# A two-level fast-multiplication block on one core: restores on ScalarE, x in seven transfers, x for results later

## The chip, the core and the metric

The kernel runs on one core of a Trainium2 chip. The core has a matrix engine (PE, TensorE), a vector engine (DVE, VectorE), an activation engine (ACT, ScalarE), a general engine (POOL, GpSimd) and SP (SyncE), which here only issues transfers. Each engine runs its own queue of instructions in order; semaphores tie the queues together. Transfers are issued by SP, ACT or POOL and carried out by DMA queues. The metric is the time on the device in microseconds, the lower the better. Three runs of the kernel before gave 2135.2, 2135.29 and 2135.4.

## The reference

x has 8 sequences of 1024 rows of 512 numbers, all float32. Cut to what matters:

```python
xn = layernorm(x)
# s: a decayed, causal product of features, three decay rates mixed by a softmax gate
q, gate = xn @ Wq, softmax(xn @ Wg)
for i in range(3):
    scores = (q @ (xn @ Wk[i]).T) * decay[i] ** expn * causal
    blended += gate[i] * (scores @ (xn @ Wv[i]))
s = blended @ Wo * out_scale
# g: a gated feed-forward part; every weight is one of 16 numbers, picked by an index
h = silu(xn @ lut[gate_idx].T) * (xn @ lut[up_idx].T)     # 1376 wide
g = silu(h @ lut[down_idx].T)
return x + s * g
```

## The kernel before

**Phase 1** works through the sequences 0 to 7. It normalizes x, computes the gated product in 8 chunks a sequence (`project`, `chunks`), and beside it builds the feed-forward weights. Everything that phase 2 needs is written to DRAM: the transposed xn of each sequence with some sums of its blocks (`xs_d`), the blended features (`bl_d`), and the weights with their sums (`quad_d`, `wgu_d`, `wd_d`, `wdl_d`, `wdt_d`).

**Phase 2** does the three feed-forward products and the result, one sequence after the other. Its products use the Winograd form of fast multiplication (7 products of half size instead of 8) on two levels: an outer step k in 1 to 7, and inside it an inner step i in 1 to 7. For each outer step the core holds seven planes of x in the tile `xs` (128 partitions, 7 outer steps, 7 planes, 256 columns): the four blocks B11, B12, B21, B22, loaded from `xs_d`, and three sums. POOL makes the sums (`sums_of_x`, L696), and one of them, B22 - B12, overwrites B12 in plane 1.

- `single` (L703 the weights `wr`, L713 the matmuls `fs`, `fsE`) computes the last 96 of the 1376 columns with plain blocks, in seven products on the outer level. In sequence 0 it comes first; in the others between the gate-up part and the down part.
- `quads` is the gate-up part: two rounds of seven nodes and then three nodes that pair two outer steps, (1, 6), (5, 7) and (2, 3), with `Fourth` for outer step 4. A `Node` loads its weights `wq` (L754, L757) into a ring of three slots, multiplies (L763), and DVE and ACT empty the four PSUM banks. `Fourth` has its weights `w` (L799) and matmuls at L806. `Fourth` and `single` use plain B12, so `restore` (L832) fetches it back from `xs_d`, one outer step for each transfer, issued by POOL: step 4 after the second round, then 1 and 6, 5 and 7, 2 and 3 behind the three pair nodes. In `after_57` and `after_23` POOL also makes sums and the multiplications of gate and up (L919), for half 1 of the columns first, then half 0.
- `down` has seven `DownNode`s in the order 1, 5, 6, 2, 7, 4, 3, whose weights `wdd` (L1009) come into the same ring. The matmuls at L1018 are its two-level part; those at L1029 multiply the rows left over (`wdl`, L1246), which the multiplications at L919 write. DVE makes the operand sums `z`, `sx`, `sy` (L986).
- The result: `tail` (L1125) adds the last 96 columns, `result` multiplies the blended features `fbl` (L1226) by Wo (L1132), DVE scales (L1134), POOL adds x (L1136), and the rows go out (L1137, by SP in the last sequence, else by POOL). This x comes into the tiles `gx` by `load` (L1082), four transfers of 256 KB for each half of the rows; half 1 takes the room of the pair nodes' tile `u2`, half 0 that of `e5`. `load` is called at the down nodes 5 (half 1) and 2 (half 0).
- While `down` runs, `beside` loads the x of the next sequence (L686), one outer step behind each node. Only the x of sequence 0 is loaded at once, 3.5 MB in one transfer, at the start of phase 2.

**What sets the order.** A scheduler orders the instructions when the program is built. `keep_order` binds PE, DVE, ACT and POOL to the order in which the code was traced; SP is left to the scheduler apart from the very start. So SP's queue can hold a transfer ahead of others that were traced before it, and as SP issues in order, a transfer whose room is not yet free holds all that stand behind it. Hardware-issued transfers share eight semaphores in turn, so one also waits until the transfer eight places before it has landed.

At the end of phase 1 SP stores `wdl_d` (L305, behind POOL's last weight sum, L303), and ACT stores the last `bl` (L580).

Of the kernel before, what the change touches and what calls it, by code (L numbers as in the profile page):

```python
# [20 lines left out]


ENGINES = (mybir.EngineType.PE, mybir.EngineType.DVE, mybir.EngineType.Activation, mybir.EngineType.Pool)


def keep_order(tc, seen, engines=ENGINES):

    last = {}
    order = mybir.DependencyInfo(mybir.DependencyClass.NoSync, mybir.DependencyReason.DATA)
    for i in tc.nc.cur_bb.bb.instructions:  # L30
        if i.name not in seen and i.engine in engines:
            if i.engine in last:
                tc.add_manual_dep(i, last[i.engine], order, reason="traced in this order")
            last[i.engine] = i.name
# [3 lines left out]
def recurrent_block(ctx: ExitStack, tc, x, wq, wk, wv, wo, wg, decay_logits, out_scale, lut, gidx, uidx, didx, out):  # L38
# [19 lines left out]
    nc = tc.nc  # L58
    B, T, V = x.shape
# [5 lines left out]
    NC = T // P  # L65
# [22 lines left out]
    xs_d = [dram.tile([P, 14, U], F32, name=f"xsd{b}", tag=f"xsd{b}") for b in range(B)]  # L88
# [37 lines left out]
    seen = {i.name for i in nc.cur_bb.bb.instructions}  # L126
# [532 lines left out]
    X_OF = {1: 0, 2: 1, 3: 2, 5: 3, 6: 4, 7: 5, 4: 6}  # L659
    D_OF = {1: 0, 7: 1, 2: 2, 3: 3, 5: 4, 6: 5, 4: 6}  # L660
    H = U // 2
    ORDER = (1, 6, 5, 7, 2, 3, 4)

    def phase_2():
        with (
# [19 lines left out]
            def load_x(b, xs, first=0, end=7):  # L685
                nc.sync.dma_start(  # L686
                    out=xs[:, first:end, 0:4, :],
                    in_=xs_d[b][:, 2 * first : 2 * end].rearrange("p (k r) (s t) -> p k (r s) t", r=2, s=2),
                )
# [136 lines left out]
            def quads(b, xs, h, sums, at_last):  # L826


                def restore(*ks):

                    for k in ks:
                        nc.gpsimd.dma_start(out=xs[:, X_OF[k], 1, :], in_=xs_d[b][:, 2 * X_OF[k], H:])  # L832

                def two(ap):
                    return ap.rearrange("p (a t) -> p a t", a=2)
# [46 lines left out]
                def pair_steps():  # L882

                    (p1, u2), (e5, u3) = (
                        (t[:, :, :H], t[:, :, H:])
                        for t in (tmp.tile([P, 4, U], F32, name=f"{k}{b}_l", tag=k) for k in ("p1", "u2"))
                    )
                    room[0] = u3

                    def of_h(half, n):  # L890
                        r, c = divmod(n, 2)
                        t = half * U + c * H
                        return h[:, 4 * NQ + r, t : t + H]

                    def node_16(t, n):
                        nc.scalar.copy(p1[:, n], t[n][:, :H])
                        nc.vector.tensor_tensor(u2[:, n], t[n][:, H:], p1[:, n], ALU.add)

                    def node_57(t, n):
                        nc.scalar.copy(e5[:, n], t[n][:, :H])  # L900
                        nc.vector.tensor_tensor(u3[:, n], t[n][:, H:], u2[:, n], ALU.add)
                        nc.gpsimd.tensor_tensor(u2[:, n], u2[:, n], e5[:, n], ALU.add)

                    def node_23(t, n):
                        nc.vector.tensor_tensor(p1[:, n], t[n][:, :H], p1[:, n], ALU.add)
                        nc.scalar.activation(of_h(0, n), p1[:, n], AF.Silu)
                        nc.vector.tensor_tensor(of_h(1, n), t[n][:, H:], u2[:, n], ALU.add)
                        nc.scalar.activation(of_h(1, n), of_h(1, n), AF.Silu)

                    def after_57():  # L910
                        for n in (0, 3, 1, 2):
                            nc.gpsimd.tensor_tensor(e5[:, n], e5[:, n], u3[:, n], ALU.add)
                        restore(5, 7)

                    def after_23():
                        restore(2, 3)
                        for half, other in ((1, e5), (0, u3)):
                            for n in (0, 3, 1, 2):
                                nc.gpsimd.tensor_tensor(of_h(half, n), of_h(half, n), other[:, n], ALU.mult)  # L919

                    yield (1, 6), node_16, lambda: restore(1, 6)
                    yield (5, 7), node_57, after_57
                    yield (2, 3), node_23, after_23
# [144 lines left out]
            def down(b, h, h_tail, bl, ahead, beside):  # L1068
# [4 lines left out]
                order = (1, 5, 6, 2, 7, 4, 3)  # L1073
# [5 lines left out]
                def load(half, pool, tag):  # L1079
                    xr[half] = pool.tile([P, 4, V], F32, name=f"gx{b}_{half}", tag=tag)  # L1080
                    for n in range(4):
                        nc.sync.dma_start(out=xr[half][:, n], in_=x[b, ts(4 * half + n, P), :])  # L1082

                def at(c, n):
                    return c[:, n // 2, n % 2]
# [44 lines left out]
                def result(k):  # L1130
                    ps = next_bank(f"ps{b}_{k}")
                    nc.tensor.matmul(ps, lhsT=bl[:, ts(k, P)], rhs=wo_sb, start=True, stop=True)  # L1132
                    g, o = of_chunk(k)
                    nc.vector.scalar_tensor_tensor(g, wide(ps), osc, g, ALU.mult, ALU.mult)  # L1134
                    end = (b, k) == (B - 1, NC // 2 - 1)
                    (nc.vector if end else nc.gpsimd).tensor_tensor(wide(o), wide(o), g, ALU.add)  # L1136
                    (nc.sync if b == B - 1 else nc.gpsimd).dma_start(out=out[b, ts(k, P), :], in_=o)  # L1137

# [3 lines left out]
                node.fifth_copy()  # L1142
                for i, k in enumerate(order):
                    following, todo = None, []
                    if k == 5:
                        load(1, tmp, "u2")
                    if k == 2:
                        load(0, tmp2, "e5")
                    if k == 6:
                        of[7], parts = sum_of(f"sx{b}_7", "sx", a11, a21, ALU.subtract)  # L1150
                        later = [p + (ALU.subtract,) for p in parts]
                    if k == 2:
                        of[3] = s2
                        later += [
                            (o, x1, o, ALU.subtract)
                            for o, x1 in zip(
                                (s2[0][:, 0:2], s2[0][:, 2:4], s2[1]), (a12[0][:, 0:2], a12[0][:, 2:4], a12[1])
                            )
                        ]
                    if k != order[-1]:  # L1160
                        kk = order[i + 1]
                        z, todo = four_of(f"z{b}_{kk}", of[kk])
                        following = DownNode(b, kk, of[kk], z)
                    if k == 1:
                        todo += first_sums
                    if k == 6:
                        todo += later[:2]
                        later = later[2:]
                    elif k in (2, 7, 4):
                        n = 2 if k == 2 else 1  # L1170
                        todo = later[:n] + todo if k == 4 else todo + later[:n]
                        later = later[n:]

                    def some(n):
                        vector_sums(todo, n)

                    empty = empties[k]
                    node.sixth()
                    some(1)
                    node.product(0, 2)  # L1180
                    node.rest(0)
                    empty(node.t, 0)
                    some(1)
                    if following:
                        following.first()
                    else:
                        tail(4, bank("s11", f"pd{b}_4"))
                    node.seventh()
                    some(1)
                    node.product(1, 3)  # L1190
                    node.rest(1)
                    empty(node.t, 1)
                    some(1)
                    if following:
                        following.fifth()
                        following.fifth_copy()
                    else:
                        tail(5, bank("sE", f"pd{b}_5"))
                    node.rest(3)
                    empty(node.t, 3)  # L1200
                    some(1)
                    node.product(2, 4)
                    node.rest(2)
                    empty(node.t, 2)
                    some(3)
                    node = following
                    beside(k)
# [4 lines left out]
                behind = 1 if b == B - 1 else 3  # L1212
# [5 lines left out]

            more = iter(())
            xs = room_for_x(0)  # L1220
            load_x(0, xs)
            for b in range(B):
                h = hp.tile([P, 2 * NK, T], F32, name=f"h{b}", tag="h")
                h_tail = hp.tile([P, T], F32, name=f"ht{b}", tag="ht")
# [27 lines left out]
                def beside(k):  # L1252
# [9 lines left out]
                    if n > 4:  # L1262
                        some(more, 4)

                down(b, h, h_tail, bl, got, beside)

    phase_1()
    phase_2()
    keep_order(tc, seen)


# [39 lines left out]
```

## Time and profile before

| | |
|---|---|
| time, median of 3 runs | 2135.29 us (2135.2 to 2135.4) |
| time of the profiled execution | 2137.89 us |
| its span, first to last instruction | 2136.1 us |
| mean granted PE clock | 0.996 |
| PE busy | 2113.7 us, 99% |
| PE weight loads busy | 1680.5 us, 79% |
| DVE, ACT, POOL busy | 1409.4, 930.1, 1054.8 us |
| moved by DMA | 361.45 MB, mean 169 GB/s |
| chain that ended last | PE 97%, DMA 1% |

Phase 1 takes the first 603.7 us. Sequence 0's gate-up part begins at 622.5, sequence 1's at 806.7, and from there a sequence takes 188.3 us. The last matmul ends near 2124.8 and the last addition of x at 2126.65. Some groups that the change touches (columns: line, engine, operation, tiles, count, then busy us and mean ns, then idle before and who ended it):

```profile
L696 POOL TENSOR_TENSOR xs<-xs 128x256 f32<-128x256 f32 x224 | 171.2, 791 | 7.8 <-DMA bld<-bl 2.2
xs<-xsd SPq DMA_DIRECT2D x49, 512.0 KB, 7.2
gx<-in_x SPq DMA_DIRECT2D x64, 256.0 KB, 4.1
wq<-quadd SPq DMA_DIRECT2D x112, 896.0 KB, 4.5
wdd<-wdd SPq DMA_DIRECT2D x56, 896.0 KB, 4.7
```

The last four are from the page's list of transfers: tile, issuing queue, count, size of one, and the median time from issue to landing. "SPq" is SP's queue. A busy PE can hide a slow one: where PE has stood still, its clock is granted at half, which the stretches of the trace show as a lower granted clock.

### The profile page before, as it was taken

Reading aid. Unit: us, or ns where it says so; the run is one execution under the profiler, and the core shown is the slowest. Engines: PE = TensorE matmul, PEld = TensorE weight load, DVE = VectorE, ACT = ScalarE, POOL = GpSimd, SP = SyncE. Lnnn points to the kernel's source line nnn. Section 1 sums busy time; section 2 is a strip of 40 time slices with the busy share of each in tenths; the row PEclk is TensorE's granted clock in tenths of the full one; section 3 lists DMA queues with packets and bytes.
Section 4 is the critical chain, followed back from the end, with each engine's and each line's share of the span. In section 5 each row is a group of like instructions: output and inputs, shape, how many; then the busy total and the mean of one; then the engine's idle time right before and its main releaser. Section 6 shows DMA issues by size and latency. Waiting matters only on the chain.

```text
span 2136.1 us, 31153 instructions
## 1 busy us (share of the span) xinstructions
PE 2113.7 (99%) x11306; PEld 1680.5 (79%) x11306; DVE 1409.4 (66%) x2149; ACT 930.1 (44%) x2083; POOL 1054.8 (49%) x1103
## 2 busy tenths in 40 slices
PE   9999999999999999999999999999999999999997
PEld 5666666666668798888879888887978888797886
DVE  6889888669535675566567556655755665675566
ACT  3666666676434414423441442344144224414531
POOL 2654565353354627517552752655275265627532
PEclk9999999999999999999999999999999999999999
DMA  7555647574474544463454446445544644554451
GB/s 195 154 175 160 199 160 170 178 159 149 120 265 152 205 159 165 143 241 137 156 198 170 156 148 235 152 149 184 179 165 148 237 137 155 166 202 155 156 167 67
DMA packets 159183, 361.45 MB, mean 169 GB/s; under 512 B 52371, under 2 KB 83350, under 8 KB 158006
## 3 DMA queue, kind: packets, MB, share of 16 engines
q1 hardware_dynamic: 149606, 336.12, 48.6%
q0 software_dynamic: 7168, 22.03, 2.9%
q8 instruction: 90, 1.47, 0.3%
q10 hardware_dynamic: 2256, 1.32, 0.2%
q14 instruction: 63, 0.52, 0.1%
HBM read 282.87 MB, written 76.55 MB: 168 GB/s over the span
## 4 chain that ended last, share of the span: by engine, by line
PE 97%; DMA 1%; DVE 0%; POOL 0%; issue 0%; SPq 0%; ACTq 0%; ACT 0%; DVEq 0%; POOLq 0%
PE s L763 32%; PE pq L437 10%; PE pv L400 8%; PE sE L763 5%; PE s21d L1018 5%; PE s12d L1018 5%; PE s11d L1018 5%; PE po L565 4%; PE fs L713 3%; PE pd L1125 3%; PE ps L1132 3%; PE sEd L1018 2%; PE psc L543 2%; PE pu L551 2%; PE fsE L713 1%; PE pt L393 1%
## 5 line engine op out<-in xcount | busy, mean ns | idle before, releaser
L763 PE MATMUL s<-xs,wq 128*128 128x256 f32 x3264 | 731.4, 379 | 0.6 <-DMA wq<-quadd 0.6
L763 PEld LDWEIGHTS s<-xs,wq 128*128 128x128 f32 x3264 | 619.4, 190 | 96.9 <-issue 8.2
L437 PE MATMUL pq<-xnT,wqk_sb 128*128 128x512 f32 x512 | 230.3, 592 | 0.0
L786 DVE TENSOR_TENSOR s<-s,e 128x512 f32<-128x512 f32 x136 | 95.2, 700 | 204.0 <-ACT s L785 204.0
L1096 POOL TENSOR_TENSOR cu<-cu 128x256 f32<-128x256 f32 x32 | 35.1, 1098 | 312.3 <-DVE cl L1095 312.3
L400 PE MATMUL pv<-wvg_sb,xnT 128*128 128x387 f32 x512 | 177.6, 489 | 0.6 <-DMA wvg_sb<-in_wv 0.6
L696 POOL TENSOR_TENSOR xs<-xs 128x256 f32<-128x256 f32 x224 | 171.2, 791 | 7.8 <-DMA bld<-bl 2.2
L790 DVE TENSOR_TENSOR sE<-s,e 128x512 f32<-128x512 f32 x136 | 95.1, 699 | 105.9 <-PE s L763 105.9
L437 PEld LDWEIGHTS pq<-xnT,wqk_sb 128*128 128x128 f32 x512 | 92.4, 190 | 92.1 <-issue 91.8
L853 POOL TENSOR_TENSOR u<-u,e 128x512 f32<-128x512 f32 x64 | 80.0, 1271 | 149.2 <-DVE u L849 130.1
L379 POOL TENSOR_SCALAR rstd<-rstd 128x1 f32<-128x1 f32 x56 | 29.5, 526 | 228.6 <-ACT junk L378 227.8
L781 ACT COPY e<-sE 128x512 f32<-128x512 f32 x136 | 79.7, 586 | 138.5 <-PE sE L763 138.5
L763 PE MATMUL sE<-xs,wq 128*128 128x256 f32 x544 | 139.6, 379 | 0.0
L400 PEld LDWEIGHTS pv<-wvg_sb,xnT 128*128 128x128 f32 x512 | 92.7, 190 | 55.1 <-issue 2.7
L774 ACT COPY s<-s 128x512 f32<-128x512 f32 x136 | 77.5, 570 | 109.8 <-PE s L763 106.0
L785 ACT COPY s<-s 128x512 f32<-128x512 f32 x136 | 77.5, 570 | 97.8 <-PE s L763 97.8
L1018 PE MATMUL s12d<-wdd,z 128*128 128x128 f32 x896 | 118.6, 275 | 0.0
L763 PEld LDWEIGHTS sE<-xs,wq 128*128 128x128 f32 x544 | 103.4, 190 | 14.1
L1018 PEld LDWEIGHTS s12d<-wdd,z 128*128 128x128 f32 x896 | 109.3, 192 | 0.2 <-ACT s12d L1040 0.2
L857 POOL TENSOR_TENSOR h<-h,u 128x512 f32<-128x512 f32 x64 | 79.8, 1278 | 46.7 <-DVE u L864 46.5
L206 DVE TENSOR_SCALAR leaf<-idx,lut_x,lut_sb 128x1024 int32<-128x1024 int32 (+2 forms) x119 | 101.2, 876 | 0.0
L545 DVE TENSOR_TENSOR pr<-psc,w_tab 128x384 f32<-128x384 f32 x64 | 35.6, 556 | 92.3 <-PE psc L543 92.2
(237 smaller groups left out, 4292.1 us busy)
## 6 DMA issues: line engine op xcount, KB each, us to landing
wq<-quadd SPq DMA_DIRECT2D x112, 896.0 KB, 4.5
wdd<-wdd SPq DMA_DIRECT2D x56, 896.0 KB, 4.7
xs<-xsd SPq DMA_DIRECT2D x49, 512.0 KB, 7.2
wq<-quadd SPq DMA_DIRECT2D x48, 448.0 KB, 3.8
x<-in_x SPq DMA_DIRECT2D x64, 256.0 KB, 5.9
xsd<-ts SPq DMA_DIRECT2D x8, 2048.0 KB, 8.6
gx<-in_x SPq DMA_DIRECT2D x64, 256.0 KB, 4.1
out<-gx POOLq DMA_DIRECT2D x56, 256.0 KB, 2.3
```

Of the source, the lines that this page charges most:

```text
L206: nc.vector.tensor_scalar(o.bitcast(I32), iv, lut_x[:rows, k, :], lut_i[:rows, k, 0:1], ALU.bitwise_and, ALU.bitwise_xor,)
L400: nc.tensor.matmul(pv, lhsT=xnT[:, v, ts(c, P)], rhs=wvg_sb[:, v, :], start=(v == 0), stop=(v == NV - 1))
L437: nc.tensor.matmul(pq, lhsT=wqk_sb[:, v, ts(j, D)], rhs=xnT[:, v, ts(hf, U)], start=(v == 0), stop=(v == NV - 1))
L565: nc.tensor.matmul(po, lhsT=lh, rhs=rh, start=(n == 0), stop=(n == len(prods) - 1))
L696: nc.gpsimd.tensor_tensor(o, x1, x2, ALU.subtract)
L713: nc.tensor.matmul(ps, lhsT=w[:, 2 * W_OF[k] + n, :m], rhs=xs[:, X_OF[k], 2 * n : 2 * n + 2, :], start=start and n == 0, stop=stop and n == 1,
L763: nc.tensor.matmul(self.t[n][:, ts(a, H)], lhsT=self.w[:, a, (0, 1, 6, 2, 3, 4, 5)[i - 1], :], rhs=self.xs[:, X_OF[self.ks[a]], D_OF[i], : ...
L786: nc.vector.tensor_tensor(self.t[1], self.t[1], self.e, ALU.add)
L790: nc.vector.tensor_tensor(self.t[3], self.t[2], self.e, ALU.add)
L853: nc.gpsimd.tensor_tensor(o[:, n], o[:, n], other[:, n], ALU.add)
L857: nc.gpsimd.tensor_tensor(of_h(half, n), of_h(half, n), two(other[:, n]), ALU.mult)
L1018: nc.tensor.matmul(self.t[n][:, ts(a, P)], lhsT=self.lhs[i][:, e, ts(a, P)], rhs=self.w[:, e, D_OF[i], :], start=start and a == 0 and e == ...
```

## The change

It has five parts. `restore` issues from ACT's queue and fetches two outer steps in one transfer, by a slice with a step. In `after_23` half 0 is multiplied before half 1. The x of sequence 0 is loaded in seven transfers in the order in which `single` uses them. `load` is called at the down nodes 7 and 4 instead of 5 and 2, and a new function, `keep_behind`, binds these transfers behind what was traced before them on SP. In the last sequence the additions of x for results 2 and 3, not for 3 alone, are on DVE.

```diff
+def keep_behind(tc, seen, names):
+
+    last = None
+    order = mybir.DependencyInfo(mybir.DependencyClass.NoSync, mybir.DependencyReason.DATA)
+    for i in tc.nc.cur_bb.bb.instructions:
+        if i.name not in seen and i.engine == mybir.EngineType.SP:
+            if last and i.name in names:
+                tc.add_manual_dep(i, last, order, reason="behind what was traced before")
+            last = i.name
...
                 def restore(*ks):
 
-                    for k in ks:
-                        nc.gpsimd.dma_start(out=xs[:, X_OF[k], 1, :], in_=xs_d[b][:, 2 * X_OF[k], H:])
+                    some_of = slice(X_OF[ks[0]], X_OF[ks[-1]] + 1, max(X_OF[ks[-1]] - X_OF[ks[0]], 1))
+                    there = xs_d[b].rearrange("p (k r) t -> p k r t", r=2)
+                    nc.scalar.dma_start(out=xs[:, some_of, 1, :], in_=there[:, some_of, 0, H:])
...
                     def after_23():
                         restore(2, 3)
-                        for half, other in ((1, e5), (0, u3)):
+                        for half, other in ((0, u3), (1, e5)):
...
                     for n in range(4):
                         nc.sync.dma_start(out=xr[half][:, n], in_=x[b, ts(4 * half + n, P), :])
+                        held.add(nc.cur_bb.bb.instructions[-1].name)
...
-                    end = (b, k) == (B - 1, NC // 2 - 1)
+                    end = b == B - 1 and k in (2, 3)
                     (nc.vector if end else nc.gpsimd).tensor_tensor(wide(o), wide(o), g, ALU.add)
...
-                    if k == 5:
+                    if k == 7:
                         load(1, tmp, "u2")
-                    if k == 2:
+                    if k == 4:
                         load(0, tmp2, "e5")
...
             xs = room_for_x(0)
-            load_x(0, xs)
+            for k in (1, 6, 5, 2, 7, 3, 4):
+                load_x(0, xs, X_OF[k], X_OF[k] + 1)
...
+    held = set()
     phase_1()
     phase_2()
+    keep_behind(tc, seen, held)
     keep_order(tc, seen)
```

The sequences of instructions on PE, DVE, ACT and POOL are otherwise the same before and after; what changes beside these lines is SP's order, which the scheduler makes.

## The prediction

> **What bounds the kernel now.** I read the busy times first: PE is busy for 2113.7 of 2136.1 us, so what can be won is PE's 22.4 us of idleness and the time after each stall in which PE runs at half clock. Then the stretches say where these lie. Columns: stretch, its length, busy us of PE, PEld, DVE, ACT, POOL, granted clock, DMA share, GB/s.
>
> ```profile
> 603.70:622.30 18.60, 14.96 (x29) 5.55 (x30) 2.06 (x3) 4.51 (x7) 9.95 (x16) 0.82 0.78 300
> 719.90:752.20 32.30, 27.83 (x182) 24.41 (x181) 22.62 (x37) 9.30 (x25) 16.30 (x19) 0.95 0.77 281
> 1560.80:1749.10 188.30, 188.30 (x1049) 158.80 (x1049) 116.52 (x190) 71.08 (x141) 97.14 (x105) 1.00 0.51 172
> 1749.10:1938.20 189.10, 188.50 (x1049) 158.67 (x1049) 116.52 (x190) 71.07 (x141) 97.08 (x104) 1.00 0.50 172
> ```
>
> A middle sequence has no idle PE at all (third row). So only four places count: the step from phase 1 to phase 2 (first row), the end of sequence 0's gate-up part (second), a slip of 0.8 us in sequence 6 (fourth), and the tail behind the last matmul. The view of PE's waits names what ended each stall (total, times, longest):
>
> ```profile
> PE fs L713 <- DMA bld<-bl: 3.7, 1, 3.7
> PE s11d L1018 <- DMA wdd<-wdd: 2.9, 1, 2.9
> ...
> PE s L806 <- DMA w<-wgud: 0.9, 1, 0.9
> PE s11d L1029 <- POOL h L919: 0.6, 1, 0.6
> PE s L763 <- DMA wq<-quadd: 0.6, 1, 0.6
> ```
>
> The first name misleads: POOL's first sum of x starts at the same instant (607.33), so it is the landing of xs, 12.9 us after its issue. The chain of waits shows what a stall costs besides its idle time (start, length):
>
> ```profile
> 607.36 6.51 PE fs L713 x8
> 613.87 1.72 PE fsE L713 x4
> 615.59 3.43 PE fs L713 x8
> ```
>
> Eight matmuls took 6.51 us instead of 3.43: another 3.1 us. The other stall did the same (PE's timeline), where eight such matmuls elsewhere take 0.89:
>
> ```profile
> 746.05 1.84 PE L1018 MATMUL s11d<-wdd,sy 128*128 128x128 f32 x8 [2.94 <-DMA wdd<-wdd]
> 747.69 1.91 PE L1018 MATMUL s21d<-wdd,z 128*128 128x128 f32 x8
> ```
>
> **A. x of sequence 0 in seven transfers.** The edit is meant to take away 3.7 + 3.1 = 6.8 us. What decides is SP's queue, which issues in order:
>
> ```profile
> 594.06 0.56 SPq L686 DMA_DIRECT2D xs<-xsd  x1
> 605.19 0.33 SPq L305 DMA_DIRECT2D wdld<-wgu  x1
> 605.69 0.33 SPq L1245 DMA_DIRECT2D wdt<-wdtd  x1
> 606.07 1.32 SPq L754 DMA_DIRECT2D wq<-quadd  x1
> 610.45 0.32 SPq L1226 DMA_DIRECT2D fbl<-bld  x1
> 610.81 0.43 SPq L1246 DMA_DIRECT2D wdl<-wdld  x1
> 611.29 0.63 SPq L754 DMA_DIRECT2D wq<-quadd  x1
> ```
>
> In the changed program's SP order the seven transfers are not together. Four (k = 1, 6, 5, 2) stand where the one stood; then comes the store wdld, which waits for POOL's last weight sum (605.16); then k = 7, 3, 4; then fbl, whose room is free only when wdld has landed; then wdt, wdl, and only then the first gate-up weights wq, which stood ahead of fbl before. So 1.5 MB of x that crossed between 601 and 605 now crosses after 605, and the first wq is issued near 611 instead of 606.07.
>
> Working: the four transfers land by about 602.5 (2.1 MB behind the rest of wr, by the 0.30 to 0.41 MB per us of the DMA rows from 594 on). PE ends phase 1 at 603.67 and waits only for ACT's copy of bl (603.96), so it starts near 604.2 with no loss of clock. The seven products of single, 1.72 us each (row 613.87), are 12.0; the fifth needs x7. wdld moves from about 606.3 to 609.2 (0.92 MB at the 0.3 MB per us it had); the three x at 0.4 follow to 613.1, landing some 1.2 us behind their bytes: x7 at 611.6 against a need at 611.1. single ends near 616.8. Then fbl, wdt, wdl, wq are 2.56 MB at 0.39 MB per us (3.10 MB in 610 to 618): last byte 619.7. Transfers here landed 1.0 (xs) to 2.6 us (the first wq) behind their bytes by the same count; so wq lands at 620.7 to 622.3, I take 621.3. PE idles 4.5 us in front of its first gate-up matmul instead of 3.7 in front of single, and its clock drops again.
>
> Here a rule weighs in. The Trainium skill, "TensorE: Matmul & The Clock Gate" (What's actually happening), says the clock halves after an idle window of about 3.4 us and returns after about as long a busy one: a loss of 1.7 us. The rows say 3.1 after 3.69 us of idleness and 1.7 after only 2.94, below the rule's limit, so a shorter stall would not escape either. By the rule A ends at 621.3 + 1.7, by the first row at 621.3 + 3.1; before, the first gate-up matmul came at 622.46 at full clock. I take 2.4: A = **+1.2 us** (ends -0.8 and +2.9). The stall is moved, not removed.
>
> A second rule speaks against splitting: "DMA: Bandwidth & Descriptors" (Rules for kernel authors) asks for 1 MiB or more in a transfer, and its fit (Anatomy of one DMA) has 2.0 us fixed for each; in sequence, six more would cost 12 us. But from 745 to 750 this queue moved 414 GB/s out of transfers of 512 and 896 KB issued back to back, as much as out of the one large x (416 from 598 to 604), so I cost the split itself at nothing.
>
> **B. x for results later, multiplications of half 0 first, restores on ACT (sequence 0).** From 624.18 to 807.61 sequence 0 needs 183.43 us; a middle sequence without single is 188.29 - 12.04 = 176.25. So 7.2 us are lost. (1) w was issued at 719.16, behind four gx loads that waited for POOL's multiply until 717.24. It now stands before them and goes when its ring slot is free, near 715 as in sequence 1 (7.6 us ahead of use, 2.1 to land): -1.2. (2) L1029 waited for POOL's half 0: 0.6 idle. It goes, but restore (2, 3) now sits on ACT just before the copy L1040 that PE's third step needs, at 0.35 (ACT's issue of bld): -0.3. (3) The third wdd was issued at 739.08, behind gx loads waiting for POOL until 737.25. It now follows the second near 728.5, needed at 740.8, landing 4.7 to 6.8 after issue: -3.1 idle and -1.7 clock. Late next is the second wdd: its slot is w's, free near 727.7, landing 4.6 later at 732.3, needed at 732.6; it may cost up to 1. Sum: **-6.2** (ends -7.2 and -4.5).
>
> **C. The other seven sequences.** gx moves some 10 us later, past two wdd, and still lands over 20 us before its use; PE is full, so 0. POOL loses seven issues (0.74 + 1.13 + 2.19 us in sequence 0), for which nobody waits there. ACT gains four of 0.35 each; every wait they carry (weights in use, earlier restores, long-landed x) is already met, and the gap before the copy L785 behind them is 0.55 to 0.62: 0. Without that cover PE waits, as the third rival says. The slip in sequence 6 is one wq that took 8.2 us instead of 4.9 beside the same stores as before; I count half of its 0.8: **-0.4** (ends -0.8, +0.8).
>
> **D. Last sums on VectorE.** After the last matmul DVE ran L1134 for results 2 and 3 to 2125.62 and one add of 1.00 to 2126.65, beside POOL's add. Now 0.8, 0.69, 0.8, 0.69 from 2124.01, with POOL idle: 2127.0. The last add is 0.35 later, the store before it 0.6 earlier: **+0.2** (-0.1, +0.4).
>
> Sum: 1.2 - 6.2 - 0.4 + 0.2 = **-5.2 us**, made against the profiled execution (2137.89, span 2136.1), which lies 2.6 above the median of 2135.29. The same gain gives **2130.1 us**.
>
> **Rivals.**
> - *A wins as meant* (wq lands before single ends): -6 instead of +1.2, near 2122.9. For it: PE could start at 604.2. Against: SP's order and 2.56 MB in front of wq. 0.12.
> - *Half of B is lost again*, by the second wdd landing over a microsecond late behind restores and x of the next sequence, with a clock drop: -3 instead of -6.2, near 2133.3. 0.17.
> - *ACT is held by its restores.* An issue above the 0.55 us gap delays PE 32 times. At 1.0 us each, 0.45 x 32 = 14 us: 2144. It outweighs the gain from 0.72 us each, and reads as slower from 0.85. For it: POOL's issues took 0.56 to 0.74. Against: ACT's own row, 0.35. 0.08.
> - The forecast: 0.63, its own range 2127.3 to 2133.
>
> What this kernel's measurement can tell is about 0.2%, 4.3 us, so below 2131.0 is faster. Of the forecast's 0.63 some 0.46 lies there, with 0.12 of the first rival: 0.58. Slower: 0.08 and a little for the unforeseen, 0.09. The range 2125.5 to 2134 leaves out most of the first rival and the third.
>
> **What would show it.** A: fs starts near 604.2, and PE's waits name wq at the gate-up matmul (L774 of the changed file) with 4 to 5 us, with slow matmuls behind; were that wait absent, A is wrong. B: no wait on w, wdd or h in 715 to 750. C: middle sequences of 188.3; if longer, look at ACT. D: the last add ends 0.3 later.

## The result, and the profile after

The changed kernel took 2136.33 us (median of 14 runs, 2134.48 to 2139.82), the kernel before 2135.35 in the 14 runs beside it (2132.47 to 2138.97). The ratio is 1.0002, with a 95% interval of 0.9994 to 1.001: no difference that can be measured. The forecast was 2130.1. The profiled execution has a span of 2135.2 us (before 2136.1) and a mean clock of 0.999.

That nothing moved does not mean that nothing happened. PE's waits in the changed kernel (who waited for what at which line: us in total, times, longest; lines of the changed file, 11 and more above those of before):

```profile
PE fs L724 <- DMA xs<-xsd: 11.1, 8, 2.0
PE s L774 <- DMA wq<-quadd: 4.0, 1, 4.0
PE warm L352 <- POOL nhalf L141: 1.4, 1, 1.4
PE s12d L1030 <- ACT s12d L1052: 0.8, 1, 0.8
PE fs L724 <- ACT bl L577: 0.4, 1, 0.4
```

The waits for wdd, w and h in sequence 0 are gone, and so is the one in front of `single` of sequence 0. The 4.0 us for wq is the stall that the forecast saw move. The first line is new: `single` waits for its x, once in sequence 0 (0.15 us) and in each later sequence for a restore (10.9 us in all). The stretches show what that makes of a sequence (columns as in the prediction; the step to the gate-up part, sequence 0, sequence 1):

```profile
603.34:623.92 20.58, 16.10 (x38) 7.37 (x38) 2.75 (x4) 5.09 (x8) 17.38 (x26) 0.92 0.96 357
623.92:801.35 177.43, 176.59 (x1022) 154.29 (x1021) 115.85 (x186) 68.05 (x136) 81.27 (x76) 1.00 0.49 170
801.35:991.33 189.98, 188.50 (x1050) 158.71 (x1049) 116.52 (x190) 71.08 (x141) 93.19 (x98) 1.00 0.50 172
```

A middle sequence took 188.30 with PE never idle; now it takes 189.98, and PE is busy for 188.50 of it.

Set stage against stage, the two profiled executions give this. A stage ends where the row names it; "gate-up" is the first block of 20 matmuls of the gate-up part, which comes four matmuls of each kind into it.

| stage | before, us | after, us | difference | forecast |
|---|---|---|---|---|
| phase 1, to its last matmul's end | 603.66 | 603.35 | -0.3 | 0 |
| A: from there to gate-up of sequence 0 | 20.52 | 20.57 | +0.05 | +1.2 |
| B: sequence 0 | 183.43 | 177.43 | -6.0 | -6.2 |
| C: sequences 1 to 7, to the last matmul's end | 1317.15 | 1328.72 | **+11.6** | -0.4 |
| D: from there to the end of the last add | 1.89 | 2.11 | +0.2 | +0.2 |
| from there to the end of the span | 9.45 | 3.02 | **-6.4** | 0 |
| sum | 2136.1 | 2135.2 | -0.9 | -5.2 |

So there are two large terms that the forecast did not have, of opposite sign. One is in the seven later sequences, the other behind the last addition, where no engine computes any more.

**The first one, in sequence 1.** ACT's timeline of the changed kernel (start, length, instruction, idle time before it), where `single` begins at 905.71:

```profile
904.66 0.42 ACT L920 ACTIVATE h<-h 128x256 f32<-128x256 f32 x1
906.37 0.42 ACT L918 ACTIVATE h<-p_l 128x256 f32<-128x256 f32 x1 [1.30 <-DVE p_l L917]
906.70 0.42 ACT L920 ACTIVATE h<-h 128x256 f32<-128x256 f32 x1
906.79 0.37 ACTq L844 DMA_DIRECT2D xs<-xsd  x1
```

SP's timeline in the same stretch, and PE's (the products of `single`, two to a row of eight matmuls):

```profile
905.04 1.18 SPq L1021 DMA_DIRECT2D wdd<-wdd  x2
```

```profile
905.71 3.60 PE L724 MATMUL fs<-xs,wr 128*96 128x512 f32 x8
909.15 1.88 PE L724 MATMUL fsE<-xs,wr 128*96 128x512 f32 x4
912.50 3.64 PE L724 MATMUL fs<-xs,wr 128*96 128x512 f32 x8 [1.48 <-DMA xs<-xsd]
```

restore(2, 3) stands behind the last Silu in ACT's queue, and that Silu waits for DVE's `p_l`. So it goes out at 906.79, 1.1 us after `single` has begun, and it lands 5.6 us behind its issue (the view of tile `xs` in this stretch). Product 2 is the fourth of `single`, 12 matmuls in; PE is ready for it at 911.0 and gets it at 912.5. In the kernel before, POOL's timeline has the same transfers in good time:

```profile
906.01 2.79 POOL L912 TENSOR_TENSOR u_l<-u_l 128x256 f32<-128x256 f32 x4
908.73 2.19 POOL L832 DMA_DIRECT2D xs<-xsd  x4
910.93 1.42 POOL L919 TENSOR_TENSOR h<-h,u_l 128x256 f32<-128x256 f32 x2
```

There `single` began at 911.97, about 2 us after operand 2 had been issued, the restores landed in 2.3 to 2.5 us, and the two wdd went out behind them, at 911.30. In the changed kernel the two wdd are ahead, by 1.75 and 0.9 us. The experiments had to tell which part matters: the place in ACT's queue, the two wdd, or the two operands in one transfer.

### The profile page after: what moved, and what is told of

The parts are those of the page before. It is cut to its first block, busy times and chain, and to the rows that moved or that the text cites. A ratio compares the mean times of both kernels' runs of the same rounds, so it can differ in the third digit from the quotient of the medians.

```text
span 2135.2 us, 31120 instructions
## 1 busy us (share of the span) xinstructions
PE 2112.1 (99%) x11306; PEld 1678.7 (79%) x11306; DVE 1410.9 (66%) x2150; ACT 930.1 (44%) x2083; POOL 1021.3 (48%) x1046
## 3 DMA queue, kind: packets, MB, share of 16 engines
q10 hardware_dynamic: 9936, 8.66, 1.3%
## 4 chain that ended last, share of the span: by engine, by line
PE 97%; DMA 3%; DVE 0%; ACT 0%; issue 0%; SPq 0%; ACTq 0%; DVEq 0%
PE s L774 33%; PE pq L448 10%; PE pv L411 8%; PE sE L774 6%; PE s12d L1030 5%; PE s21d L1030 5%; PE s11d L1030 5%; PE po L576 4%; PE pd L1138 3%; PE ps L1145 3%; PE sEd L1030 2%; PE psc L554 2%; PE fs L724 2%; DMA xs<-xsd 2%; PE pu L562 2%; PE pt L404 1%
## 5 line engine op out<-in xcount | busy, mean ns | idle before, releaser
L785 ACT COPY s<-s 128x512 f32<-128x512 f32 x136 | 77.5, 570 | 114.3 <-PE s L774 110.9
L774 PEld LDWEIGHTS sE<-xs,wq 128*128 128x128 f32 x544 | 103.9, 191 | 14.3
```

Of the source, the lines that this page charges most:

```text
L774: nc.tensor.matmul(self.t[n][:, ts(a, H)], lhsT=self.w[:, a, (0, 1, 6, 2, 3, 4, 5)[i - 1], :], rhs=self.xs[:, X_OF[self.ks[a]], D_OF[i], : ...
```

## The experiments

Eleven kernels. A, B, C, D are the steps of the forecast. The kernel before ran beside them with medians of 2135.82, 2136.34 and 2135.83 us.

### 1. The restores back on POOL (e1_restore_pool)

```diff
-                    some_of = slice(X_OF[ks[0]], X_OF[ks[-1]] + 1, max(X_OF[ks[-1]] - X_OF[ks[0]], 1))
-                    there = xs_d[b].rearrange("p (k r) t -> p k r t", r=2)
-                    nc.scalar.dma_start(out=xs[:, some_of, 1, :], in_=there[:, some_of, 0, H:])
+                    for k in ks:
+                        nc.gpsimd.dma_start(out=xs[:, X_OF[k], 1, :], in_=xs_d[b][:, 2 * X_OF[k], H:])
```

> The changed kernel with restore alone undone: POOL issues it again, one outer step for each transfer. Theory (the restores on ACT come too late for single in sequences 1 to 7): PE's 11.1 us of waits of fs for xs fall below 0.5 us, a middle sequence takes 188.3 us instead of 190.0, and the time is about 2125 us, 11 below the changed kernel and 10 below the one before. Rival (the later sequences are longer because the x for results now crosses beside wdd and the next x): the sequences stay at 190 and the time near 2136.

Measured: 2129.47 us (2128.28 to 2130.14), ratio 0.9965 (0.9952 to 0.9977). The wait of `single` for its x is 0.4 us in all, the sequences are 188.29 again. From sequence 1's gate-up to the last matmul's end e1 takes 1316.3 us, 12.4 less than the changed kernel. The table has +11.6 because the kernel before lost 0.8 us in sequence 6 (189.13), the slip that the prediction names, and neither of the other two did. So the restores' new place costs some 12 us. But the time fell by only 6.9 us against the changed kernel; at the end of the program 4.5 us are lost again (under 6).

### 2. restore(2, 3) on ACT, but earlier (e2_restore_early)

```diff
                     def after_23():
-                        restore(2, 3)
...
                     node.seventh()
+                    if node.ks == (2, 3):
+                        restore(2, 3)
```

> The changed kernel with one line moved: restore(2, 3) stays on ACT as one transfer of two operands, but is traced behind the seventh product of the node (2, 3), ahead of the last three pairs of silu. Theory (late because ACT's queue stood at the last silu): it is issued some 3.3 us before single begins instead of 1.1 after, lands 2.5 to 3.5 us later instead of 5.6 because the two wdd transfers are not yet in front of it, the waits of fs vanish, and the time is about 2125 us. Rival (a transfer of two operands from ACT is slow by itself): it still takes 5 to 6 us to land; PE might then just be spared, but the landing time shows it.

Measured: 2125.71 us (2122.93 to 2127.5), ratio 0.9947 (0.9934 to 0.9959). ACT issues it at 904.61, with `single` from 907.85 and the two wdd from 907.18 on; ACT's restores in this stretch land in 2.7 to 3.3 us, no PE wait for `xs` is left, and sequences 1 to 5 last 188.29 (the sixth 189.14, with 0.6 us of waiting for wq as in the kernel before). ACT's queue and two operands in a transfer do no harm by themselves; what decides is when restore(2, 3) is issued, here ahead of the two wdd.

### 3. One operand to a transfer (e7_restore_single)

```diff
-                    nc.scalar.dma_start(out=xs[:, some_of, 1, :], in_=there[:, some_of, 0, H:])
+                    for k in ks:
+                        nc.scalar.dma_start(out=xs[:, X_OF[k], 1, :], in_=xs_d[b][:, 2 * X_OF[k], H:])
```

> The changed kernel with ScalarE's restores as one operand to a transfer, in the same places. If the stall in single comes from when the pair is issued (behind the last Silu on ScalarE) and from the two wdd of 896 KB on the way beside it, operand 2 still lands about 5 us behind its issue: PE waits about 1 to 1.5 us for xs in sequences 1 to 7, these last 189.4 to 190.0, and the time is within 3 us of the changed kernel's 2136. If it comes from putting two operands into one transfer, operand 2 alone lands 2.5 to 3.5 us behind its issue, the wait is under 0.3 us, the middle sequences are 188.3 long and the time is 2125 to 2129.

Measured: 2135.93 us (2133.43 to 2139.3), ratio 0.9998 (0.999 to 1.0006), as the changed kernel. PE waits 9.3 us for these transfers in seven sequences, which last 189.6 to 190.1; the longest landing is again 5.6 us. Pairing the operands is not the cause.

### 4. The two wdd held until the restore has landed (e11_wdd_behind)

```diff
+                    restored[b] = nc.cur_bb.bb.instructions[-1].name
...
+                    if k == 1 and b > 0:
+                        landed = mybir.DependencyInfo(mybir.DependencyClass.Sync, mybir.DependencyReason.DATA)
+                        tc.add_manual_dep(nc.cur_bb.bb.instructions[-1], restored[b], landed, reason="restored")
```

> The changed kernel, restore(2, 3) where it was on ScalarE, but in sequences 1 to 7 the first wdd of 896 KB is issued only when restore(2, 3) has landed, and the second behind it. If the two wdd that went out 1.7 us ahead of restore(2, 3) are what made it land 5.6 us behind its issue, it lands 2.3 to 3.5 us behind it now, well before product 2 of single needs it (5.15 us into single); PE waits for no xs, the middle sequences last 188.3 and the time is 2124 to 2128. If the landing is slow for another reason (ScalarE's queue, or the place behind the Silu), it stays near 5.6, the wait of 1.5 us stays, sequences last 189.9 and the time stays at 2136 or rises, should the later wdd hold PE.

Measured: 2123.92 us (2122.19 to 2124.65), ratio 0.9941 (0.9927 to 0.9955). In sequence 1 ACT's restore and SP's wdd, and PE behind them:

```profile
905.98 0.37 ACTq L844 DMA_DIRECT2D xs<-xsd  x1
```

```profile
908.84 0.80 SPq L1022 DMA_DIRECT2D wdd<-wdd  x2
```

```profile
904.91 3.60 PE L724 MATMUL fs<-xs,wr 128*96 128x512 f32 x8
908.34 1.88 PE L724 MATMUL fsE<-xs,wr 128*96 128x512 f32 x4
910.06 3.60 PE L724 MATMUL fs<-xs,wr 128*96 128x512 f32 x8
```

The restore is issued 1.07 us into `single`, as late as in the changed kernel (1.08), at the same place behind the Silu. It lands in 2.7 us instead of 5.6 (2.6 to 2.8 in all seven sequences), and PE does not stop: 905.98 + 2.7 is 908.7, and product 2 begins at 910.06. The later wdd do not make PE wait.

The view of the DMA queues shows what held the restore (queue, kind: packets, MB, share of the 16 engines). q1 carries SP's transfers, q10 ACT's: q10 moved 1.32 MB before and 8.66 after, and the 56 operands restored are 7.3. First the changed kernel from 907 to 910.5, then from 910.5 to 912.5:

```profile
q1 hardware_dynamic: 220, 1.46, 100.4%
```

```profile
q10 hardware_dynamic: 272, 0.26, 37.2%
q1 hardware_dynamic: 42, 0.19, 22.6%
```

Up to 910.5, 3.7 us behind its issue, no packet of the restore had moved; then it crossed behind the last of the wdd. In e11, from 905.5 to 909, it has the engines to itself:

```profile
q10 hardware_dynamic: 272, 0.26, 25.8%
```

So the stall takes both: the restore is late **and** 1.8 MB of wdd is ahead of it on the way. The late issue alone (1.07 + 2.7) fits into the 5.15 us that `single` leaves. The wdd ahead of a restore that is not late was not tried; by these figures, an estimate, a landing of 5.6 us would still do if the issue came 0.5 us or more ahead of `single`.

### 5. One part of the change alone (e3, e4, e5, e6)

e3 takes only the new `restore`, e4 only the later x for results with half 0 first, e5 only the seven transfers, e6 only the last sums; e3's diff is that of `restore` shown with the change, and the others':

```diff
 # e4_only_gx
-                    if k == 5:
+                    if k == 7:
                         load(1, tmp, "u2")
-                    if k == 2:
+                    if k == 4:
                         load(0, tmp2, "e5")
...
+    keep_behind(tc, seen, held)
 # e5_only_x7
-            load_x(0, xs)
+            for k in (1, 6, 5, 2, 7, 3, 4):
+                load_x(0, xs, X_OF[k], X_OF[k] + 1)
 # e6_only_last
-                    end = (b, k) == (B - 1, NC // 2 - 1)
+                    end = b == B - 1 and k in (2, 3)
```

> The kernel before with the new restore alone. Theory: seven waits of fs for xs of 1.5 to 2 us each, 188.3 becomes 190 in each later sequence, and the time is 2135 + 11 = 2146 us, slower by 0.5%. Rival (the loss needs the other edits): no such waits, 2135 us.

> The kernel before with two edits alone: the x for results loaded later and held on SP, and half 0 multiplied first. Theory: sequence 0 from its first gate-up part to that of sequence 1 falls from 183.4 to about 177.3 us, PE's waits for w, wdd and h vanish, and the time is 2135.3 - 6 = 2129.3 us. Rival (this gain needs the restores off POOL, because the next x in front of the third wdd waits for them): a wait for wdd stays, and the gain is 3 us or less.

> The kernel before with the seven transfers of x alone. The forecast's step A says +1.2 us (its ends -0.8 and +2.9); the two profiles, compared from the end of phase 1 to the first gate-up block, gave +0.1. So within 0.15% of the kernel before: the wait for xs in front of single (3.7 us, behind bl) gone, a wait of 3.5 to 4.5 us for wq in front of the first gate-up matmul in its place, the first gate-up matmuls at half clock, and sequences 0 to 7 as long as before (183.4 and 188.3). Rival (A wins as meant): the wait for wq under 1 us and the time 6 us shorter.

> The kernel before with the last sums of results 2 and 3 on VectorE alone. The forecast's step D says +0.2 us, from the last matmul's end to the last add's end 2.1 us where the kernel before has 1.9; nothing else moves, so the time is the same within the interval. Rival: the last store starts later by more than the add does, or the end of the program shortens because GpSimd is idle (its 9.1 us behind the last store in the profile of the kernel before, 2.7 in the profile of the changed one): then 1 us or more on either side.

| | time, us | ratio to before (95%) | A, us | sequence 0 | sequences 1 to 6, each |
|---|---|---|---|---|---|
| before, profiled | | | 20.52 | 183.43 | 188.29, the sixth 189.13 |
| e3, restores | 2139.36 | 1.0017 (1.001 to 1.0024) | 20.17 | 178.67 | 189.87 to 192.28 |
| e4, x for results | 2130.7 | 0.9969 (0.9959 to 0.998) | 20.57 | 177.70 | 188.29 |
| e5, seven transfers | 2137.66 | 1.0005 (0.9997 to 1.0014) | 20.51 | 185.18 | 188.29 |
| e6, last sums | 2134.2 | 0.9994 (0.9986 to 1.0002) | 19.24 | 181.40 | 188.28 to 188.30 |

e4: sequence 0 is 5.7 us shorter in its profile and the time about 6.6 us (0.31% of 2135.82, from 4.3 to 8.8; the medians lie 5.1 apart). B holds, alone. PE no longer waits for w, wdd or h there; the stall in front of `single` is left:

```profile
PE fs L724 <- DMA bld<-bl: 3.6, 1, 3.6
```

e5: A alone gives nothing, and the wait for `wq` is there, 3.6 us, as in the changed kernel. In its profiled run phase 1 was 4.1 us longer, with a wait of 2.3 us of its own there, so only the stage is compared.

e3 lost less than was expected of it. The stall is there in full:

```profile
PE fs L713 <- DMA xs<-xsd: 11.3, 7, 2.1
```

But sequence 0 was 4.8 us shorter too. The edit also changed SP's order, which the scheduler makes: the third wdd, which in the kernel before stood behind the gx loads that waited for POOL, follows the second. SP's timeline, before and in e3:

```profile
739.08 0.43 SPq L1009 DMA_DIRECT2D wdd<-wdd  x1
```

```profile
722.53 8.56 SPq L1010 DMA_DIRECT2D wdd<-wdd  x3
```

PE no longer waits for wdd there. POOL itself is no sooner: its last multiplication ends 113.1 us behind the first block of 20 in both. So most of what B repairs in sequence 0 this edit repairs as well, and the two gains don't add. With +13.7 us in the later sequences (one of them took 192.28) and -4.5 at the end (under 6), e3's profile makes +4.4; the times show +3.6 (2.1 to 5.1).

How much sequence 0 wins depends on PE's clock behind its stall for wdd. Before, the stall was 2.94 us, the clock in the two microseconds behind it 0.57, and the sequence took 183.43. In e5 and e6, which do not touch it, these were 2.69, 0.50 and 185.18 (of which 1.0 is A's half clock running over into the first block of 20), and 2.58, 1.00 and 181.40.

### 6. The end of the program (e9_pool_early, e10_pool_late)

From the last addition to the end of the span there were 9.45 us before and 3.02 after. SP's waits in the last 11 us of the kernel before, and of the changed one, at the last line of the program:

```profile
SPq L1307 <- PEq L1307: 6.8, 2, 6.3
SPq L1307 <- DMA out<-gx: 1.6, 2, 1.0
```

```profile
SPq L1323 <- DMA out<-gx: 1.1, 1, 1.1
SPq L1323 <- PEq L1323: 0.7, 2, 0.5
```

The name PEq is only that of the last to arrive. The view of that last line lists a DRAIN instruction on every engine and semaphores behind it, and POOL's is the long one (count, shortest/median/longest in ns, first and last start); before, e9 (which comes below) and after:

```profile
L1307 POOLq DRAIN  x3: 40/102/10539, 2124.8 to 2135.9; - x3
```

```profile
L1335 POOLq DRAIN  x3: 40/102/8342, 2109.6 to 2118.5; - x3
```

```profile
L1323 POOLq DRAIN  x3: 40/93/5982, 2128.4 to 2134.9; - x3
```

It starts with POOL's last addition, which is the last row of POOL's timeline, and the span ends some 0.7 us behind it. That addition before, in e6 and after:

```profile
2124.84 1.26 POOL L1136 TENSOR_TENSOR gx<-gx,cl 128x512 f32<-128x512 f32 x1 [0.45 <-DVE cl L1134]
```

```profile
2119.56 1.27 POOL L1136 TENSOR_TENSOR gx<-gx,cl 128x512 f32<-128x512 f32 x1 [0.45 <-DVE cl L1134]
```

```profile
2128.43 1.28 POOL L1149 TENSOR_TENSOR gx<-gx,cl 128x512 f32<-128x512 f32 x1 [0.45 <-DVE cl L1147]
```

They end at 2126.10, 2120.83 and 2129.71; the spans end at 2136.1, 2130.8 and 2135.2. That is 10.0, 10.0 and 5.5 us. The first two have 112 transfers issued by POOL, the third 56 (`out` of seven sequences). Two kernels, made from the fastest one (7. below), were to tell whether the number counts or what was issued last:

```diff
 # e9_pool_early; e10_pool_late has b > 3
+                    if b < 4:
+                        for k in ks:
+                            nc.gpsimd.dma_start(out=xs[:, X_OF[k], 1, :], in_=xs_d[b][:, 2 * X_OF[k], H:])
+                        return
```

> The fastest version (e8_best) with the 28 restores of sequences 0 to 3 on GpSimd, one operand each; those of sequences 4 to 7 stay on ScalarE. Asked is the end of the program, from the end of GpSimd's last add to the end of the span: it was 10.0 us in all five profiles of kernels with 112 transfers issued by GpSimd (restores and stores), and 5.5 in all five with 56 or 57. If it grows with the number of transfers that GpSimd has issued in all (81 ns for each), it is 7.7 us here, with 85. If it depends on what was issued last on that queue, it is 5.5. If one restore on that queue is enough, 10.0.

> The same with the 28 restores of sequences 4 to 7 on GpSimd and those of 0 to 3 on ScalarE. From GpSimd's last add to the end of the span: 7.7 us if it grows with the number of transfers (85, as in the run beside it), 10.0 if it depends on what was issued last or if one restore is enough.

| kernels | transfers issued by POOL | POOL's last add to the end, us | POOL's DRAIN, us |
|---|---|---|---|
| before, e1, e4, e5, e6 | 112 | 10.0 to 10.1 | 10.54 to 10.55 |
| e9 and e10 | 85 | 7.85 and 7.85 | 8.34 and 8.34 |
| e8 | 57 | 5.5 | 6.06 |
| after, e2, e3, e7, e11 | 56 | 5.4 to 5.5 | 5.96 to 5.98 |

It grows with the number, about 82 ns for each transfer (4.57 us of DRAIN over 56), wherever in the program it was issued. It does not go by the bytes: e8's 57th transfer has 896 KB, seven times a restored operand, and adds 0.09. (e9 and e10 took 2120.54 and 2121.45 us, one run each.) What POOL does inside the DRAIN no row says.

This explains what two steps were worth. C took 56 transfers from POOL: 4.5 us less at the end. D took POOL's last addition away: it ended 1.34 us behind the last matmul before (2126.10 against 2124.76) and 0.36 ahead of it after (2129.71 against 2130.07), so the end came 1.7 us sooner, although the last addition of all came 0.2 later. e6, with D alone, measured 2.1 us less by the medians, with an interval that reaches across no change.

### 7. What is best (e8_best)

To the early restore of e2 it adds what A lacked: SP's queue free in front of the first `wq`.

```diff
-                defer(3, lambda: nc.sync.dma_start(out=wdl_d, in_=t[:, : 7 * V // 2]))
+                defer(3, lambda: nc.gpsimd.dma_start(out=wdl_d, in_=t[:, : 7 * V // 2]))
...
                 quads(b, xs, h, more, no_sums if b else at_last)
+                if b == 0:
+                    for o, i in (
+                        (bl, bl_d[b]),
+                        (wd_tail[: OCH[-1][1], :], wdt_d),
+                        (wd_left, wdl_d.rearrange("p (k o) -> p k o", o=H)),
+                    ):
+                        nc.sync.dma_start(out=o, in_=i)
+                        held.add(nc.cur_bb.bb.instructions[-1].name)
```

> The changed kernel with restore(2, 3) issued behind the seventh product (as in the fastest run so far, 2125.7) and with the stall of step A taken up: the store wdld goes out by GpSimd's queue, and fbl, wdt and wdl of sequence 0 stand behind the gate-up weights in SyncE's queue, so that x7, x3, x4 and the first wq are held by nothing on that queue. If the order of that queue is the cause of A's stall (4.0 us idle and about 2 at half clock), PE's wait for wq in front of the first gate-up matmul falls under 1 us and the time is 2119 to 2122. Rival 1: wr and x fill the transfers' bandwidth anyway, wq lands no earlier than about 618.5, and half or less is won (2123 to 2125). Rival 2: GpSimd's issue of the store holds its sums of x, single waits for them, and nothing is won or some lost (2125 to 2128).

Measured: 2119.22 us (2119.12 to 2119.51, four runs), ratio 0.992 (0.9907 to 0.9932). SP's queue:

```profile
594.54 3.32 SPq L697 DMA_DIRECT2D xs<-xsd  x7
598.32 26.68 SPq L765 DMA_DIRECT2D wq<-quadd  x4
```

In the changed kernel four x, the store wdld, three x, fbl, wdt and wdl stood there, and then the first `wq`:

```profile
604.87 0.32 SPq L316 DMA_DIRECT2D wdld<-wgu  x1
...
610.97 5.70 SPq L765 DMA_DIRECT2D wq<-quadd  x3
```

PE, from the last product of `single` on, in e8:

```profile
614.86 1.88 PE L724 MATMUL fs<-xs,wr 128*96 128x512 f32 x4
616.58 1.03 PE L774 MATMUL s<-xs,wq 128*128 128x256 f32 x4
```

In the changed kernel those were:

```profile
614.44 1.88 PE L724 MATMUL fs<-xs,wr 128*96 128x512 f32 x4
620.30 2.08 PE L774 MATMUL s<-xs,wq 128*128 128x256 f32 x4 [3.97 <-DMA wq<-quadd]
```

Four matmuls in 1.03 us instead of 2.08: no stall, and no loss of clock behind it. The stage takes 14.3 us instead of 20.6 (gate-up at 618.47, phase 1's end at 604.14).

## Why the prediction was wrong, step by step

**The step that failed is C**: "every wait they carry (...) is already met, and the gap before the copy L785 behind them is 0.55 to 0.62: 0". Both hold. ACT was not held by an issue of 0.37 us, and the restores waited for nothing of their own. The step asked what the four issues cost ACT. It did not ask what stands ahead of restore(2, 3) on ACT, Silus that wait for DVE, nor when its data has to be there, nor what would be ahead of it on the way. A and B follow each transfer that moves on SP's queue to its landing and to who needs it; C did not do so for ACT's. In its place the runs show +11.6 us, or 12.4 against e1, about 1.8 in each of seven sequences. That the place costs this is shown by e1 and e2, that it takes the two wdd as well by e11, that the pairing has no part in it by e7. The half of the slip in sequence 6 that C counted as won was won whole (0.8), which the sum hides; no run shows why.

**The rival "ACT is held by its restores"** named the right engine and the right sign with the wrong mechanism: it priced the length of an issue, from 0.72 us on, and the issue is 0.37.

**A** was right in kind. The stall moved to the first gate-up matmul, 4.0 us with matmuls at half speed behind it, for the reason given, the order of SP's queue. `wq` came at 620.3, just ahead of the span of 620.7 to 622.3; +1.2 was +0.05, inside its ends. e5 shows it alone, and e8 shows that the queue's order was the cause. The rival "A wins as meant" needed e8's edits.

That the sum came so near is in part luck. e6, which does not touch A, took 19.24 us for it, 1.3 less than the kernel before: the eight matmuls behind a stall of 3.74 us took 5.20 there, and 6.51 before.

Of the two rules weighed there, the Trainium skill, "TensorE: Matmul & The Clock Gate" (What's actually happening), has the clock at half after an idle window of about 3.4 us and back after a busy one as long; the 1.7 us lost is an estimate from that. The changed kernel met it: behind its stall of 3.97 us it took 3.62 us from its first gate-up matmul to the block of 20 (620.30 to 623.92), e8 without a stall 1.89 (616.58 to 618.47). But e5, behind a stall of 3.64, took 3.78 to the block and 5.46 for it, where e8's block took 4.44: 2.9 us lost. Together with the stalls for wdd under 5, of 2.58 us with no loss and of 2.69 with one, this says that these runs give no fixed price for a stall; what sets it stays open.

The Trainium skill, "DMA: Bandwidth & Descriptors" (Anatomy of one DMA), gives its 2.0 us fixed for each transfer as a fit to transfers that GpSimd issues; the seven are SP's. In e8 they were issued in 3.32 us and the last landed 12.5 us behind the first issue, where the single large one took 12.9 before, and PE was never short of x. So costing the split at nothing held.

**B** was right: -6.0 against -6.2 (its parts add to -6.3), and -5.7 in e4. The rival that half of it would be lost to the second wdd did not happen.

**D** was right to the last addition (+0.2) and wrong in taking that for the end. POOL's last addition sets it.

**The end of the program** was in no step. That SP waits 6.3 us at the last line stood in the trace of before; the sum took only differences between stages and so carried it along as a constant. It was worth -6.4 us.

The forecast's -5.2 missed +12.0 in C and -6.4 at the end; with -1.1 in A, +0.2 in B and -0.3 in phase 1 this makes the -0.9 of the two profiles. By these two profiles the change would have been slower by 5.5 us without the gain at the end, which nobody looked for: that the times came out the same is luck.

## What to carry to other kernels

When an issue moves to another engine, look at three times: when it goes out behind what stands ahead of it there, what other queues have sent by then, and when the data is needed; in this case the busy queue did no harm (e2), the late issue did. When a change brings nothing, cut both traces into stages up to the very end of the span, since a loss and a gain can cancel. Experiments with one part alone can share a gain (e3 and e4 in sequence 0), so also take a part out of the whole.

## What was not expected of the hardware

- POOL's DRAIN at the end of the program got longer by 82 ns for each transfer that POOL had issued: 10.54 us with 112, 8.34 with 85, 5.97 with 56, even if the last of those in question (e9) was issued in the first half of phase 2.
- A restore of 256 KB from ACT's queue landed 5.6 us behind its issue when two transfers of 896 KB had left SP's queue 1.75 and 0.9 us before, and 2.7 us when they had not. Being on another queue did not let it pass: its first packet moved more than 3.7 us behind its issue.
- PE's clock was 0.50 behind a stall of 2.69 us (e5) and 1.00 behind one of 2.58 (e6), in front of the same matmuls.
- e8 ran four times within 0.4 us, while the kernel before scattered from 2133.2 to 2142.9 in the 35 runs beside it. Stalls with a loss of clock are gone from e8, and those may be what scatters; this was not tested.
